# Layer 0 attention: 26 of 96 banks of probabilities transposed by VectorE's blocks and DRAM, the other evictions on ScalarE, one more step of lag

## The chip, the core and the metric

The kernel runs on one core of a Trainium2 chip. The metric is the device time of that core in microseconds (us), as a median over runs. A profile is one execution recorded by the hardware profiler. The core's engines appear in it as PE (TensorE matmuls), PEld (TensorE weight loads), DVE (VectorE), ACT (ScalarE) and POOL (GpSimd); SP is the engine whose queue issues most DMAs. All data are float32.

## The reference

Two transformer layers run over x of shape (4, 256, 512). Each layer is attention and a linear map, each with a residual and a layer norm. The change is in layer 0's attention: 32 query heads of 16 dimensions, 8 key and value heads (4 query heads share one), causal.

```python
q = (x @ Wq + bq).reshape(B, S, 32, 16).transpose(0, 2, 1, 3)      # B, S = 4, 256
k, v = (x @ Wk + bk), (x @ Wv + bv)                                # 8 heads, each repeated 4 times
scores = jnp.einsum('bhqd,bhkd->bhqk', q, k) / 4
scores = jnp.where(causal, scores, NEG)
p = jax.nn.softmax(scores, axis=-1)
out = jnp.einsum('bhqk,bhkd->bhqd', p, v)
x = layernorm(x + out.reshape(B, S, 512) @ Wo + bo)
x = layernorm(x + x @ W0.T + bias)        # W0 from scales and integer codes
```

Layer 1 has 32 query heads and 8 key heads of 128 dimensions with a bias by distance, and a linear map with small integer weights.

## The kernel before

**Layer 0 attention** is 64 steps (b, qt, h, i): 4 sequences b, 2 query tiles qt of 128 rows, 2 halves h, 4 values of i. A step does four heads (G = 4). For qt = 0 a query tile sees one key tile of 128 columns, for qt = 1 two.

`begin0` starts a step. Score matmuls (L482) fill a PSUM tile `sc` (two of these exist). VectorE adds the mask to the diagonal (L487) and takes the negated maximum (L490). ScalarE makes four exponentials with their sums (L274). `divide0` then treats the step before: VectorE takes the reciprocal of its sums (L279), pinned in program order, and GpSimd multiplies the probabilities `pr` by it (L282). There are six `pr` buffers.

`transpose0` brings the probabilities of a step into `prT`, with keys on the partitions, because the output matmul contracts over keys. `transposed_probabilities` does this for each key tile: four TensorE transposes (L297) fill one PSUM bank `pt`, and `evacuate` copies the bank into `prT`. `evacuate` alternates between VectorE (L100) and ScalarE (L102), and all evictions of the layer that call it share that one turn: the transposed inputs xT, x1T, x2T and the attention output oT too. With 32 steps of one bank and 32 of two, layer 0 has 96 such banks. `pt` banks come from a ring of three PSUM banks, which the projections use too.

`end0` acts on the last i of a group (b, qt, h): output matmuls (L531) over `prT` of the whole group, into the bank `o`; after h = 1 `o` is copied to `oT` and `tail0` (output projection L438, norm, linear map L455, norm) is queued.

`run` orders the work. In iteration n it calls, in this order, `before`, `begin0` of step n, `fill`, `transpose0` of step n - lag, and `end0` of step n - lag - more. In layer 0 lag is 3 and more is 2. `fill` advances the queued tails and the projections of the next sequence (L386 keys, L399 queries, L414 values), which are spread over the steps. The order of the calls is a priority for the scheduler that orders each engine's instructions; `keep_in_program_order` pins an instruction to its traced place on its engine, and each engine executes in the order it is given. So the work around the change is: PE takes scores, filling work, transposes and output matmuls in turn, and softmax runs on the other engines a few steps ahead of the transposes.

**Layer 1** (not changed in what it does) sends most of its probabilities another way, `transposed_by_blocks`. VectorE's stream transpose (L308) transposes every 32 x 32 block of `pr` into `blocks`; four DMAs on SP (L314), one for each 32 partitions, write `blocks` to a DRAM tile `way` so that the blocks come to their transposed places; one DMA (L318) reads `way` into `prT`. There writes and read are traced together.

Of the kernel before, what the change touches and what calls it, by code (L numbers as in the profile page):

```python
# [12 lines left out]
F32 = mybir.dt.float32  # L13
# [7 lines left out]
P = 128  # L21
B, S, D = 4, 256, 512
NTT = B * S // P
NC = D // P
NKV, G = 8, 4
# [34 lines left out]
def block_kernel(  # L60
# [20 lines left out]
    nc = tc.nc  # L81
    slopes = [float(s) for s in alibi_slopes()]

    def pool(stack, name, bufs=1, **kw):
        return stack.enter_context(tc.tile_pool(name=name, bufs=bufs, **kw))
# [9 lines left out]
    def evacuate(dst, src):  # L95

        if not last:
            turn[0] ^= 1
        if turn[0] and not last:
            nc.vector.tensor_copy(dst, src)  # L100
        else:
            nc.scalar.copy(dst, src)  # L102
# [20 lines left out]
    a0 = pool(la, "a0", 2, side="right")  # L123
# [7 lines left out]
    def bank_t(name):  # L131
        return ring[0].tile([P, 4, P], F32, tag=ring[1], name=name)
# [156 lines left out]
        pr = sp.tile([P, G, 2 * P], F32, tag="pr", name=f"pr_{name}", bufs=bufs)  # L289
        return nm, sums, pr  # L290

    def transposed_probabilities(name, pr, parts):

        for kt, dst in parts:
            pt = bank_t(f"pt_{name}_{kt}")
            for i in range(G):
                nc.tensor.transpose(pt[:, i, :], pr[:, i, ts(kt, P)], ident)  # L297
            evacuate(dst, pt.rearrange("p i (j q) -> p i j q", q=32))

    def transposed_by_blocks(sp, name, pr, nt, dst):  # L300

        blocks = sp.tile(
            [P, 2, 4, G, 32], F32, tag="blocks", name=f"blocks_{name}", bufs=1
        )
        for kt in range(nt):
            nc.vector.transpose(  # L308
                blocks[:, kt].rearrange("p j h q -> p h j q"),
                pr[:, :, ts(kt, P)].rearrange("p h (j k) -> p h j k", k=32),  # L310
            )
        way = dram.tile([2, 4, 32, 4, G * 32], F32, tag="way", name=f"way_{name}")
        for i in range(4):
            nc.sync.dma_start(  # L314
                way[0:nt, :, :, i, :].rearrange("t j k f -> k (t j) f"),
                blocks[32 * i : 32 * i + 32, 0:nt].rearrange("k t j h q -> k (t j) (h q)"),
            )
        nc.sync.dma_start(  # L318
            dst.rearrange("p t j h q -> p t (j h q)"),
            way[0:nt].rearrange("t j k i f -> (j k) t (i f)"),  # L320
        )
# [174 lines left out]

    open0 = {}
    undivided = []

    def divide0():  # L500


        if undivided:
            divided(*undivided.pop(), True)

    def transpose0(b, qt, h, i, pr):
        name = f"0_{b}_{qt}_{h}_{i}"
        if i == 0:
            open0["p", h] = a0.tile(
                [P, 2, G, 4, 4, 32], F32, tag="prT", name=f"prT0_{b}_{qt}_{h}"  # L510
            )
        prT = open0["p", h]
        transposed_probabilities(
            name,
            pr,
            [(kt, prT[:, kt, i].rearrange("p j n q -> p n j q")) for kt in range(qt + 1)],
        )
        return prT

# [36 lines left out]
    def fill():  # L556
# [6 lines left out]
        [(b, qt, h, i) for b in range(B) for qt in range(2) for h in range(2) for i in range(G)],  # L563
        begin0,
        transpose0,
        end0,
        before0,
        fill,
        lag=3,
        more=2,  # L570
        rest=divide0,
    )
# [179 lines left out]
    s1 = pool(ctx, "s1", 2)  # L752
# [233 lines left out]
    def transpose1(kv, b, qt, pr):  # L986
        name = f"1_{kv}_{b}_{qt}"
        nt = qt + 1
        if kv == NKV - 1:
            prT = s1.tile([P, 2, 4, G, 32], F32, tag="prT", name=f"prT_{name}")  # L990
            transposed_probabilities(
                name, pr, [(kt, prT[:, kt].rearrange("p j h q -> p h j q")) for kt in range(nt)]
            )
            return prT
        prT = s1.tile([P, 2, 4, G, 32], F32, tag="prT", name=f"prT_{name}")
        transposed_by_blocks(s1, name, pr, nt, prT[:, 0:nt])
        return prT

    def end1(kv, b, qt, prT):
# [40 lines left out]
    def fill1():  # L1040
# [9 lines left out]
        [(kv, b, qt) for kv in range(NKV) for b in range(B) for qt in range(2)],  # L1050
        begin1,
        transpose1,
        end1,
        before1,
        fill1,
        lag=1,
# [38 lines left out]
```

## Time and profile before

| | |
|---|---|
| median of 3 runs | 973.45 us (973.12 to 974.13) |
| the profiled execution | 973.24 us |
| its span, first to last instruction | 971.0 us |
| mean granted TensorE clock | 0.993 of full speed |
| layer 0's score matmuls (L482), first and last start | 15.2 and 255.2 us |
| layer 0's output matmuls (L531), first and last start | 40.7 and 277.3 us |
| layer 0's transposes of probabilities (L297), first 300 us | 384 matmuls, 96 banks |
| evictions of these banks | VectorE 43, ScalarE 53 |
| stream transposes (L308), all in layer 1 | 84 |

How to read it: a row of a group names line, engine, operation, the tiles written and read, shapes and count; then the busy time in us, the mean duration of one in ns, and after the second bar the engine's idle time before these instructions with what ended most of it. A matmul's duration includes its latency; successive ones overlap, so their spacing is read from start to start. In a table of windows each line is a stretch of the span, with each engine's busy us and instruction count, then the granted clock, the busy share of the DMA engines and their GB/s.

### The profile page before, as it was taken

Reading aid. Unit: us, or ns where it says so; the run is one execution under the profiler, and the core shown is the slowest. Engines: PE = TensorE matmul, PEld = TensorE weight load, DVE = VectorE, ACT = ScalarE, POOL = GpSimd, SP = SyncE. Lnnn points to the kernel's source line nnn. Section 1 sums busy time; section 2 is a strip of 40 time slices with the busy share of each in tenths; the row PEclk is TensorE's granted clock in tenths of the full one; section 3 lists DMA queues with packets and bytes.
Section 4 is the critical chain, followed back from the end, with each engine's and each line's share of the span. In section 5 each row is a group of like instructions: output and inputs, shape, how many; then the busy total and the mean of one; then the engine's idle time right before and its main releaser. Section 6 shows DMA issues by size and latency. Waiting matters only on the chain.

```text
span 971.0 us, 11394 instructions
## 1 busy us (share of the span) xinstructions
PE 940.3 (97%) x3593; PEld 557.4 (57%) x3593; DVE 619.9 (64%) x1291; ACT 316.5 (33%) x1194; POOL 445.1 (46%) x461
## 2 busy tenths in 40 slices
PE   7999999999899999999999999999999999999996
PEld 5645555554344445666666666666666666666652
DVE  3876867777632446766666676666676667666566
ACT  2664564555511002333212122121222212223442
POOL 2463552644436313443534543534633643556732
PEclk9999999999899999999999999999999999999998
DMA  9300000000020010444443444333453334342001
GB/s 283 138 1 1 0 1 1 1 1 1 1 86 1 22 44 23 108 131 130 117 133 99 116 124 130 119 83 108 124 143 97 113 90 123 99 118 69 1 23 65
DMA packets 76418, 74.45 MB, mean 77 GB/s; under 512 B 5957, under 2 KB 52678, under 8 KB 76358
## 3 DMA queue, kind: packets, MB, share of 16 engines
q1 hardware_dynamic: 75542, 72.28, 26.1%
q10 hardware_dynamic: 816, 1.44, 0.5%
q8 instruction: 29, 0.48, 0.2%
q14 instruction: 31, 0.25, 0.1%
HBM read 49.58 MB, written 24.12 MB: 76 GB/s over the span
## 4 chain that ended last, share of the span: by engine, by line
PE 85%; POOL 7%; DVE 4%; ACT 1%; DMA 1%; issue 1%; SPq 0%; POOLq 0%; DVEq 0%
PE p_q L632 18%; PE po L875 15%; PE sc L962 8%; PE o L1002 8%; PE p_k L632 5%; PE p_v L632 5%; PE o L531 5%; PE sc L482 4%; PE pt L297 4%; PE pq L399 3%; PE py L438 3%; PE pf L455 3%; PE py L836 3%; POOL pr L282 1%; POOL to L861 1%; ACT pr L274 1%
## 5 line engine op out<-in xcount | busy, mean ns | idle before, releaser
L274 ACT ACTIVATE pr<-sc,nm 128x256 f32<-128x256 f32 (+1 forms) x512 | 208.9, 419 | 374.7 <-DVE nm L978 279.2
L282 POOL TENSOR_TENSOR pr<-pr,sums 128x512 f32<-128x512 f32 (+1 forms) x128 | 189.9, 1484 | 240.4 <-DVE sums L279 235.7
L970 DVE SCALAR_TENSOR_TENSOR sc<-table,sc 128x128 f32<-128x128 f32 (+1 forms) x256 | 86.0, 356 | 34.8 <-PE sc L962 32.5
L274 ACT ACTIVATION_READ_ACCUMULATOR pr<-sc,nm 128x1 f32 x512 | 103.5, 202 | 0.0
L962 PEld LDWEIGHTS sc<-kT,qT 128*128 128x128 f32 x512 | 82.4, 191 | 35.1 <-issue 29.2
L962 PE MATMUL sc<-kT,qT 128*128 128x256 f32 (+1 forms) x512 | 95.2, 327 | 0.0
L1002 PE MATMUL o<-prT,v 128*128 128x512 f32 x192 | 92.9, 593 | 0.0
L646 DVE TENSOR_TENSOR qT<-p_q,qT 128x512 f32<-128x512 f32 x96 | 64.6, 686 | 35.6 <-PE p_q L632 34.8
L308 DVE STREAM_TRANSPOSE blocks<-pr 128x512 f32<-128x512 f32 x84 | 57.6, 698 | 45.6 <-POOL pr L282 45.6
L978 DVE TENSOR_REDUCE nm<-sc 128x2 f32<-128x512 f32 (+1 forms) x128 | 70.0, 550 | 1.5
L297 PEld LDWEIGHTS pt<-ident,pr 128*128 128x128 f32 x432 | 49.6, 142 | 33.0 <-issue 18.2
L297 PE MATMUL pt<-ident,pr 128*128 128x128 f32 x432 | 62.8, 280 | 5.7 <-POOL pr L282 5.3
L490 DVE TENSOR_REDUCE nm<-sc 128x4 f32<-128x512 f32 (+1 forms) x64 | 61.0, 953 | 1.1
L482 PE MATMUL sc<-kT,qT 32*128 32x256 f32 (+1 forms) x256 | 59.9, 533 | 1.6 <-ACT pr L274 1.6
L487 DVE TENSOR_TENSOR sc<-sc,causal 128x512 f32<-128x512 f32 x64 | 44.3, 692 | 26.4 <-PE sc L482 26.2
L875 PE MATMUL po<-wo,so 128*128 128x256 f32 x224 | 58.0, 382 | 2.1 <-POOL so L612 2.1
L632 PE MATMUL p_q<-x2T,ws_q 128*128 128x512 f32 x128 | 59.8, 593 | 0.0
L632 PE MATMUL p_q<-xt,ws_q 128*128 128x512 f32 x128 | 57.8, 593 | 1.8 <-POOL ws_q L615 1.8
L875 PE MATMUL po<-wo,o 128*128 128x256 f32 x224 | 57.7, 381 | 0.0
L632 PE MATMUL p_q<-x2T,wq 128*128 128x512 f32 x128 | 57.6, 593 | 0.0
L102 ACT COPY o<-o 128x512 f32<-128x512 f32 x29 | 17.0, 585 | 124.5 <-PE o L1002 124.5
L875 PE MATMUL po<-to,so 128*128 128x256 f32 x224 | 53.3, 381 | 0.9 <-POOL so L615 0.9
(155 smaller groups left out, 1435.6 us busy)
## 6 DMA issues: line engine op xcount, KB each, us to landing
way<-blocks SPq DMA_DIRECT2D x112, 128.0 KB, 2.5
prT<-way SPq DMA_DIRECT2D x28, 512.0 KB, 3.7
wq<-in_L_attn_w_qkv_dram SPq DMA_DIRECT2D x8, 1024.0 KB, 5.3
wo<-in_L_attn_w_o_dram SPq DMA_DIRECT2D x8, 1024.0 KB, 5.4
way<-blocks SPq DMA_DIRECT2D x112, 64.0 KB, 1.8
prT<-way SPq DMA_DIRECT2D x28, 256.0 KB, 2.7
wk<-in_L_attn_w_qkv_dram SPq DMA_DIRECT2D x4, 512.0 KB, 4.0
wv<-in_L_attn_w_qkv_dram SPq DMA_DIRECT2D x2, 1024.0 KB, 6.3
```

The lines of the kernel that those rows point to most:

```text
L274: nc.scalar.activation(pr[:, i, 0:w], sc, AF.Exp, bias=nm[:, i : i + 1], accum_out=sums[:, i : i + 1])
L282: nc.gpsimd.tensor_tensor(pr[:, :, 0:w], pr[:, :, 0:w], sums.unsqueeze(2).to_broadcast([P, G, w]), ALU.mult)
L297: nc.tensor.transpose(pt[:, i, :], pr[:, i, ts(kt, P)], ident)
L482: nc.tensor.matmul(sc[:, j, :, 0:w], qT[rows, i, ts(qt, P)], kT[rows, :, 0:w], start=True, stop=True)
L490: nc.vector.tensor_reduce(nm, scf[:, :, 0:w], AX.X, ALU.max, negate=True)
L632: nc.tensor.matmul(bank, fixed, moving, start=(c == 0), stop=(c == 1))
L646: add = lambda dst, a, b: nc.vector.tensor_tensor(dst, a, b, ALU.add)
L875: nc.tensor.matmul(bank[:, ts(n, HALF)], left[:, c, :], right[:, c, :], start=(c == 0), stop=(c == 1),)
L962: nc.tensor.matmul(sc[:, m, 0:w], qT[:, 2 * j + m, b * S + qt * P : b * S + (qt + 1) * P], kT[:, b * S : b * S + w], start=True, stop=True,)
L970: nc.vector.scalar_tensor_tensor(sc[:, m, 0:w], table[:, 2 * P - w :], slopes[kv * G + 2 * j + m], sc[:, m, 0:w], ALU.mult, ALU.add,)
L978: nc.vector.tensor_reduce(nm[:, 2 * j : 2 * j + 2], sc[:, :, 0:w], AX.X, ALU.max, negate=True)
L1002: nc.tensor.matmul(o, v1[:, 2 * b + kt, ts(kv, P)], prT[:, kt].rearrange("p j h q -> p h j q"), start=(kt == 0), stop=(kt == qt),)
```

## The change

In layer 0, for every (b, qt) from (0, 1) to (2, 1), key tile 0 of some steps no longer goes through TensorE: for qt = 1 the steps with i = 0, 1, 2 (their second key tile stays on TensorE), for qt = 0 the steps with i = 0 and 2. That makes 3 x 2 x 3 + 2 x 2 x 2 = 26 banks. They take `transposed_by_blocks` with one key tile, from two buffers of one tile each (layer 1 keeps one buffer of two tiles). In layer 0 VectorE's transpose is pinned in program order. The four writes are traced at once; the read is returned as a function, which the next step's `transpose0` calls after its own writes, and which is pinned on SP's queue. All other banks except those of (0, 0) are copied by ScalarE alone instead of in turns. The lag is 4 steps instead of 3.

```diff
-    def transposed_probabilities(name, pr, parts):
+    def transposed_probabilities(name, pr, parts, copy=evacuate):
...
-            evacuate(dst, pt.rearrange("p i (j q) -> p i j q", q=32))
+            copy(dst, pt.rearrange("p i (j q) -> p i j q", q=32))
...
-    def transposed_by_blocks(sp, name, pr, nt, dst):
+    def transposed_by_blocks(sp, name, pr, nt, dst, room):
...
-            [P, 2, 4, G, 32], F32, tag="blocks", name=f"blocks_{name}", bufs=1
+            [P, room, 4, G, 32], F32, tag="blocks", name=f"blocks_{name}", bufs=2 // room
...
-            nc.vector.transpose(
+            ins = nc.vector.transpose(
...
+            if room == 1:
+                tc.keep_in_program_order(ins)
...
-        nc.sync.dma_start(
+        return lambda: nc.sync.dma_start(
             dst.rearrange("p t j h q -> p t (j h q)"),
...
+    unread = []
...
     def transpose0(b, qt, h, i, pr):
...
         prT = open0["p", h]
+        rest = range(qt + 1)
+        reads = list(unread)
+        unread.clear()
+        if (0, 0) < (b, qt) < (B - 1, 0) and i in ((0, 2), (0, 1, 2))[qt]:
+            rest = rest[1:]
+            unread.append(transposed_by_blocks(a0, name, pr, 1, prT[:, 0:1, i], 1))
+        for read in reads:
+            tc.keep_in_program_order(read())
+        copy = evacuate if (b, qt) == (0, 0) else nc.scalar.copy
         transposed_probabilities(
-            name,
-            pr,
-            [(kt, prT[:, kt, i].rearrange("p j n q -> p n j q")) for kt in range(qt + 1)],
+            name, pr, [(kt, prT[:, kt, i].rearrange("p j n q -> p n j q")) for kt in rest], copy
         )
         return prT
...
-        lag=3,
+        lag=4,
...
-        transposed_by_blocks(s1, name, pr, nt, prT[:, 0:nt])
+        transposed_by_blocks(s1, name, pr, nt, prT[:, 0:nt], 2)()
```

## The prediction

> **What bounds the kernel now.** The page first, for the whole; then the table of windows, cut at the first score matmul of each (b, qt) stretch of layer 0, for where each engine is full; then PE's order of time; then the rows by form for prices.
>
> ```profile
> PE 940.3 (97%) x3593; PEld 557.4 (57%) x3593; DVE 619.9 (64%) x1291; ACT 316.5 (33%) x1194; POOL 445.1 (46%) x461
> ...
> PE 85%; POOL 7%; DVE 4%; ACT 1%; DMA 1%; issue 1%; SPq 0%; POOLq 0%; DVEq 0%
> ```
>
> PE is busy 97% of the span and is 85% of the chain that ended last. A busy PE need not be at its peak, so I go to the stretches (columns: PE, PEld, DVE, ACT, POOL busy, then the granted clock and DMA). Six of the nine:
>
> ```profile
> 38.60:67.60 29.00, 28.51 (x147) 15.48 (x146) 22.43 (x40) 18.51 (x70) 16.14 (x11) 1.00 0.00 1
> 67.60:101.00 33.40, 33.24 (x166) 18.36 (x166) 22.66 (x48) 18.40 (x79) 13.80 (x14) 1.00 0.01 1
> 101.00:134.00 33.00, 32.52 (x157) 17.34 (x156) 25.92 (x46) 18.06 (x69) 17.46 (x13) 1.00 0.00 1
> ...
> 200.50:230.00 29.50, 28.68 (x142) 13.37 (x142) 20.61 (x44) 17.51 (x75) 13.34 (x13) 1.00 0.00 1
> 230.00:256.00 26.00, 25.14 (x110) 11.31 (x109) 19.99 (x35) 15.95 (x62) 13.39 (x10) 1.00 0.00 0
> 256.00:297.00 41.00, 37.03 (x125) 16.36 (x124) 13.97 (x27) 8.92 (x25) 19.29 (x15) 0.92 0.15 52
> ```
>
> From 38.6 to 134 PE idles 1.1 us in 95.4. VectorE is at 77%, 68% and 79% in these three, ScalarE at 55 to 64%, and the DMA engines stand still. PE sets the pace wherever the change takes banks away; VectorE is next. The last stretch is different: PE idles 4.0 us and the clock falls.
>
> PE's timeline gives what a bank of four transposes really holds of PE (start, us, what):
>
> ```profile
> 140.38 1.04 PE L297 MATMUL pt<-ident,pr 128*128 128x128 f32 x8
> 141.35 0.70 PE L482 MATMUL sc<-kT,qT 32*128 32x256 f32 x4
> ...
> 146.54 0.66 PE L297 MATMUL pt<-ident,pr 128*128 128x128 f32 x4
> 147.12 0.69 PE L482 MATMUL sc<-kT,qT 32*128 32x256 f32 x2
> ```
>
> Eight hold it 141.35 - 140.38 = 0.97 us, four 147.12 - 146.54 = 0.58. So one bank beside another costs about 0.39 to 0.44 (start to start of single transposes is 0.109 us, four are 0.436), and a bank that is a group of its own costs 0.58, because the change of operand shape is paid too. The rows of the first 300 us:
>
> ```profile
> L297 PE MATMUL pt<-ident,pr 128*128 128x128 f32 x384 | 56.0, 280 | 3.6 <-POOL pr L282 3.2 <-DVE v L422 0.2
> L102 ACT COPY prT<-pt 128x512 f32<-128x512 f32 x53 | 30.9, 591 | 30.2 <-PE pt L297 30.1
> L100 DVE COPY prT<-pt 128x512 f32<-128x512 f32 x43 | 29.0, 675 | 7.8 <-PE pt L297 7.8
> ```
>
> Its mean of 280 ns is latency, not spacing; 384 matmuls are 96 banks.
>
> **The change part by part.** *PE loses 26 banks.* In (0,1), (1,1), (2,1) the blocks take key tile 0 of i = 0, 1, 2 for two h: 3 x 6 = 18 banks, each beside a second bank that stays: 18 x 0.436 = 7.8 us. In (1,0), (2,0) they take the only bank of i = 0, 2: 2 x 4 = 8 groups: 8 x 0.58 = 4.6 us. Together 12.5 us, all on PE, at full clock, in the stretches where PE hardly idles. This is the main term: -12.5.
>
> *A rule against it.* The Trainium skill, "VectorE: DVE Perf Modes", sections "The three transpose paths" and "Rules for kernel authors", says to give a 128x128 transpose to TensorE if PSUM may receive it, and prices one (bf16) at 390 ns there and 311 ns on VectorE, in 32x32 blocks only. By those prices a bank of four would free 1.56 us of PE, 40 us in all, and cost VectorE 1.24 us instead of a 0.60 us copy, +17 us on the engine next in load. This case's row for a whole bank on VectorE is shorter:
>
> ```profile
> L308 DVE STREAM_TRANSPOSE blocks<-pr 128x512 f32<-128x512 f32 x82 | 56.2, 698 | 44.2 <-POOL pr L282 44.1
> ```
>
> The row is layer 1's; it covers a bank in 698 ns, and in VectorE's timeline the next instruction starts 0.60 us after it, as after a copy. I use 0.58 and 0.436 for PE and 0.60 for VectorE.
>
> *VectorE.* It takes 26 transposes and gives up nearly all of its 43 prT copies, since every eviction after (0,0) goes to ScalarE; the four banks of (0,0) that may fall to it stay. Some 39 x 0.60 = 23 us go, 26 x 0.60 = 16 us come. Within the five changed stretches about half of their 64 banks were VectorE's, so there it is nearly a swap: same work in less time. (1,1) then runs at about 25.9/30.4 = 85% and (0,1) at 85%. In b = 3 (24 banks, no blocks) VectorE loses about 7 us of the 41 in its two stretches.
>
> *ScalarE.* 96 - 26 - 4 = 66 copies for 53: +13 x 0.59 = 7.7 us, nearly all in b = 3, where it goes from 33.5 of 55.5 us to some 40. A copy queued there delays the exponentials behind it, and through them the score tiles PE waits for; at 72% load I count that as covered.
>
> *Wait for the probabilities.* The pinned transpose heads VectorE's queue until GpSimd has divided; behind it wait the next step's mask and maximum, so exponentials and scores. Layer 1's row shows 44.2 us of such waits in 82. Here the tile is four steps old (about 15 us), while its reciprocal is issued one step on and the division takes 1.1 or 1.9 us, so I take zero.
>
> *DMAs.* Each bank adds four writes and a read on SP, idle in layer 0 between its loads near 23 us and the value weights at 282 us; engines at 0.00. Layer 1's same sizes:
>
> ```profile
> way<-blocks SPq DMA_DIRECT2D x112, 64.0 KB, 1.8
> prT<-way SPq DMA_DIRECT2D x28, 256.0 KB, 2.7
> ```
>
> Issue of four writes takes 1.8 us on SP (timeline of layer 1), landing 1.8 more, then the read waits for its turn one step on (3.8 us) and lands in 2.7: some 8 us after the transpose. The last block of a group is i = 2, and its output matmul is traced three steps later, over 11 us. Cover about 3 us or more; nothing on the path. The bounds: 0, and the rival below.
>
> *Lag 4.* Moves each transpose one step later behind the scores. It removes GpSimd waits of PE: 1.0 us near 227 and, at the drain, where PE waits 2.60 us at 256.8 for a division, one more group of eight transposes (0.97 us) stands in front. -2.0. Six pr buffers leave one step of slack instead of two: zero.
>
> *New stalls.* Stretch (3,1), with VectorE at 77% and little filling work, idles PE 0.86 us in 26; before that with 79% and filling work 0.48 in 33. At 85% I charge the worse rate, doubled, to the three qt = 1 stretches (some 90 us): 90 x 2 x 0.033 = 6 as the upper bound, zero as the lower, and take 2, nearer the filled stretch. VectorE's relief in b = 3 and two copies (1.2 us) fewer ahead of the last softmax may give some back; I leave that in the range.
>
> Sum: -12.5 - 2.0 + 2.0 = -12.5 us. On the profiled execution of 973.24 (span 971.0 and 2.2 around it): 960.7. The median before is 0.2 above that execution, so 960.9.
>
> **The clock at the drain.** In 252 to 264 the granted clock is 0.76 and in 264 to 276 0.95:
>
> ```profile
> 252.00:264.00 12.00, 9.40 (x42) 4.55 (x42) 8.09 (x16) 6.00 (x20) 4.33 (x3) 0.76 0.00 1
> ```
>
> That is 0.24 x 12 + 0.05 x 12 = 3.5 us of lost clock, less half of what fell into the wait, about 2.9. The Trainium skill, "TensorE: Matmul & The Clock Gate" (Part 4 and "Why this matters for your kernels"), allows idle gaps to about 3 us and says transposes do not count as busy. The gap here is 2.60 us, shorter than allowed, and mostly transposes precede it. By the gap alone a 1.6 us wait is safe and 2.9 us come back; by the second sentence an extra group of transposes does not help. I take no gain and keep -2.9 for the range.
>
> **The rivals.**
> 1. *VectorE and the ScalarE queue become the bound* (0.14). The stalls reach their upper bound of 6 and lag 4 gains nothing: -12.5 + 6 = -6.5, 967. For: 85% in order. Against: PE idles only 0.5 us at 79%.
> 2. *The drain clears* (0.16). The short wait vanishes, the clock stays up: another -0.6 - 2.9, and VectorE's relief in b = 3 repays about 1.2: 956.2.
> 3. *Slower: the round trip through DRAM ends late* (0.05). Ten groups hold blocks, and each group's output matmul holds PE for the read. With 14.5 us gained, it decides at 1.45 us per group. If SP's pinned read waits behind the next step's writes, and these for a VectorE running a step and a half late, 8 us become 13.5, about 2 late: +20, net +5.5, 979. Against: VectorE's lag behind PE is seldom over 3 us here.
> 4. *No effect* (0.03): PE's time refills with waits for exponentials. 973. Against: such waits of PE's score matmuls come to 1.6 us.
>
> The likeliest (0.62) has its own range, 957 to 964.
>
> **How the numbers follow.** A measurement tells about 0.2% (1.9 us) from no change. Faster is cases 1, 2 and the likeliest, 0.92; same 0.03; slower 0.05. For 8 in 10 the range takes the likeliest, most of case 2 and the better part of case 1: 954.5 to 967.5.
>
> **What would show it.** L297 falls from 384 to 280 matmuls in layer 0, the prT copies of VectorE from 43 to about 4, ScalarE's rise to about 66; 26 more stream transposes and 26 more reads of 256 KB. The stretches (0,1) to (2,1) shrink by 2 to 3 us each with PE idle below 1 us; the chain stays on PE. I am wrong if output matmuls (L531) wait on a DMA, if PE waits for exponentials or banks grow by several us, or if the drain grows by more than it should.

## The result and the profile after

The changed kernel takes 973.75 us (median of 12 runs, 971.51 to 975.65) against 973.08 us before: a ratio of 1.0005, 95% interval 0.9997 to 1.0014. I had forecast 960.9 us; nothing that can be measured was gained. What each engine has to do changed as forecast. The rows of the first 300 us and the page's DMA rows after:

```profile
L297 PE MATMUL pt<-ident,pr 128*128 128x128 f32 x280 | 40.2, 277 | 1.1 <-POOL pr L282 1.1
L298 ACT COPY prT<-pt 128x512 f32<-128x512 f32 x62 | 35.3, 596 | 45.1 <-PE pt L297 45.1
L308 DVE STREAM_TRANSPOSE blocks<-pr 128x512 f32<-128x512 f32 x26 | 18.1, 698 | 0.1
```

```profile
way<-blocks SPq DMA_DIRECT2D x216, 64.0 KB, 1.8
prT<-way SPq DMA_DIRECT2D x54, 256.0 KB, 2.7
```

PE does 104 matmuls fewer (384 to 280), ScalarE 62 prT copies by the new line L298 and four more by `evacuate`, and VectorE 26 stream transposes at 698 ns that wait for nothing (0.1 us). Writes and reads land in 1.8 and 2.7 us as in layer 1. But:

```profile
PE 932.1 (96%) x3489; PEld 546.9 (56%) x3489; DVE 613.3 (63%) x1273; ACT 324.4 (33%) x1212; POOL 444.2 (46%) x461
...
PE 82%; POOL 7%; DVE 5%; ACT 4%; issue 2%; DMA 1%; SPq 0%; POOLq 0%; DVEq 0%; ACTq 0%
```

PE works 8.2 us less and the span is 0.5 us longer: ScalarE's part of the chain grew from 1 to 4%. Where this falls is shown by the table of windows, cut at the first score matmul of each (b, qt) stretch. These are (1,0), (1,1), (2,1), the first part of (3,1), and the rest; the last cut is at 253.3 us, while scores of (3,1) still run to 261.1, so the last two lines are not the windows of before:

```profile
64.30:98.80 34.50, 32.04 (x151) 16.50 (x150) 22.64 (x47) 18.11 (x78) 13.04 (x13) 0.95 0.36 88
98.80:133.80 35.00, 32.37 (x133) 15.56 (x132) 25.38 (x45) 18.48 (x71) 17.89 (x13) 0.95 0.27 67
...
166.30:202.60 36.30, 33.67 (x135) 16.01 (x134) 25.44 (x45) 18.55 (x71) 17.91 (x13) 0.91 0.26 64
...
229.70:253.30 23.60, 19.75 (x89) 8.19 (x88) 18.29 (x32) 17.73 (x67) 13.84 (x10) 1.00 0.00 1
253.30:297.50 44.20, 43.11 (x157) 20.58 (x158) 13.03 (x27) 13.41 (x34) 19.98 (x16) 0.96 0.14 48
```

Stretch (1,1) took 33.0 us before with PE idle 0.5 us at full clock. Now, with less for PE to do, it takes 35.0 us with PE idle 2.6 us and the granted clock at 0.95. VectorE's load in it is 73%, not the 85% I feared. Stretch (3,1) lost most: its scores start from 229.7 to 261.1 us, 31.4 us, for 25.2 us before (230.0 to 255.2). PE's own list of waits (15 to 283 us; total, times, longest) names what it waits for, before and after:

```profile
PE sc L482 <- ACT pr L274: 1.6, 4, 0.4
```

```profile
PE sc L484 <- ACT pr L274: 12.2, 14, 1.7
```

Two pairs of these waits stand near 120 and 188 us. Here is ScalarE near 120 us, first before the change, then after (the sums between the exponentials are left out):

```profile
119.73 1.08 ACT L102 COPY prT<-pt 128x512 f32<-128x512 f32 x2
121.46 0.58 ACT L102 COPY oT<-o 128x512 f32<-128x512 f32 x1 [0.64 <-PE o L531]
121.94 0.48 ACT L274 ACTIVATE pr<-sc,nm 128x256 f32<-128x256 f32 x1
```

```profile
120.21 0.59 ACT L298 COPY prT<-pt 128x512 f32<-128x512 f32 x1
120.68 0.51 ACT L274 ACTIVATE pr<-sc,nm 128x256 f32<-128x256 f32 x1
...
121.14 0.50 ACT L274 ACTIVATE pr<-sc,nm 128x256 f32<-128x256 f32 x1
...
121.59 0.51 ACT L274 ACTIVATE pr<-sc,nm 128x256 f32<-128x256 f32 x1
...
122.04 0.51 ACT L274 ACTIVATE pr<-sc,nm 128x256 f32<-128x256 f32 x1
...
122.49 0.63 ACT L102 COPY oT<-o 128x512 f32<-128x512 f32 x1
```

And PE at the same places, before and after:

```profile
119.50 1.91 PE L531 MATMUL o<-prT,v 128*32 128x512 f32 x8
121.34 1.13 PE L482 MATMUL sc<-kT,qT 32*128 32x512 f32 x4
122.40 3.70 PE L438 MATMUL py<-wop,oT 128*128 128x512 f32 x8
```

```profile
117.14 1.91 PE L544 MATMUL o<-prT,v 128*32 128x512 f32 x8
120.38 1.13 PE L484 MATMUL sc<-kT,qT 32*128 32x512 f32 x4 [1.34 <-ACT pr L274]
122.70 1.12 PE L484 MATMUL sc<-kT,qT 32*128 32x512 f32 x2 [1.19 <-ACT pr L274]
123.75 5.40 PE L440 MATMUL py<-wop,oT 128*128 128x512 f32 x8
```

Before, ScalarE took oT 0.05 us after the output matmuls had ended (121.41), and PE went from one group of scores straight to the output projection `py`. After, the output matmuls end at 119.05, but oT stands behind a prT copy and the four exponentials of one more step and starts at 122.49, 3.44 us late. PE cannot do `py`; what stands ahead of it is half of the next scores, which wait for those same exponentials. Then `py` takes 5.40 us for 3.70: the trace has half the clock granted from 124.6 us, for 3.41 us. The same happens near 187 and 250 us: oT of (1,0), (2,0) and (3,0), the three on ScalarE, is late by 3.44, 3.44 and 3.23 us; the five on VectorE are not.

So theory A was that the softmax chain through VectorE had become the bound; the rivals were the longer lag (B), ScalarE's copies as such (C), PE's own order (D), and the pinned block transposes (E). Out of the first runs came F: it is the place of oT in ScalarE's queue.

### The profile page after: what moved, and what is told of

Same layout as the page of the kernel before. It is cut to its first block, busy times and chain, and to the rows that moved or that the text cites. A ratio compares the mean times of both kernels' runs of the same rounds, so it can differ in the third digit from the quotient of the medians.

```text
span 971.5 us, 11444 instructions
## 1 busy us (share of the span) xinstructions
PE 932.1 (96%) x3489; PEld 546.9 (56%) x3489; DVE 613.3 (63%) x1273; ACT 324.4 (33%) x1212; POOL 444.2 (46%) x461
## 4 chain that ended last, share of the span: by engine, by line
PE 82%; POOL 7%; DVE 5%; ACT 4%; issue 2%; DMA 1%; SPq 0%; POOLq 0%; DVEq 0%; ACTq 0%
PE p_q L645 18%; PE po L888 15%; PE sc L975 8%; PE o L1015 8%; PE p_k L645 5%; PE p_v L645 5%; PE sc L484 4%; PE py L440 4%; PE o L544 3%; ACT pr L274 3%; PE pf L457 3%; PE py L849 3%; PE pt L297 2%; PE pq L401 2%; POOL to L874 1%
## 5 line engine op out<-in xcount | busy, mean ns | idle before, releaser
L274 ACT ACTIVATION_READ_ACCUMULATOR pr<-sc,nm 128x1 f32 x512 | 105.9, 207 | 0.0
L308 DVE STREAM_TRANSPOSE blocks<-pr 128x512 f32<-128x512 f32 x110 | 75.7, 698 | 45.7 <-POOL pr L282 45.6
L484 PE MATMUL sc<-kT,qT 32*128 32x256 f32 (+1 forms) x256 | 62.3, 535 | 12.5 <-ACT pr L274 12.2
L888 PEld LDWEIGHTS po<-to,so 128*128 128x128 f32 x224 | 42.2, 190 | 16.3 <-issue 8.8
L297 PEld LDWEIGHTS pt<-ident,pr 128*128 128x128 f32 x328 | 37.2, 141 | 24.3 <-issue 15.4
```

The lines of the kernel that those rows point to most:

```text
L274: nc.scalar.activation(pr[:, i, 0:w], sc, AF.Exp, bias=nm[:, i : i + 1], accum_out=sums[:, i : i + 1])
L308: ins = nc.vector.transpose(blocks[:, kt].rearrange("p j h q -> p h j q"), pr[:, :, ts(kt, P)].rearrange("p h (j k) -> p h j k", k=32),)
L484: nc.tensor.matmul(sc[:, j, :, 0:w], qT[rows, i, ts(qt, P)], kT[rows, :, 0:w], start=True, stop=True)
L888: nc.tensor.matmul(bank[:, ts(n, HALF)], left[:, c, :], right[:, c, :], start=(c == 0), stop=(c == 1),)
```

## The experiments

All ratios are to the kernel before, on the same chip. "oT late" is worked out from each trace: the start of each oT copy minus the end of the last output matmul ahead of it, summed over the eight. "Clock lost" is (1 - mean granted clock) x span, an upper bound for what the falls cost, the ends of the span included. The profile is one execution, so the last two columns show direction, not a law. Executions of one kernel differ with the clock: four of e2's six took 962.1 to 962.5 us at a mean clock of 0.997 to 0.998, the other two 967.6 and 967.9 us at 0.992.

| run | what it is | us | ratio (95%) | oT late | clock lost |
|---|---|---|---|---|---|
| before | | 973.1 to 973.5 | 1 | 1.0 | 6.8 |
| after | the change | 973.75 | 1.0005 (0.9997 to 1.0014) | 10.5 | 10.7 |
| e1 | before, lag 4 | 972.03 | 0.9989 (0.9983 to 0.9996) | 2.4 | 1.9 |
| e7 | e1, ScalarE copies | 982.54 | 1.0113 (1.0092 to 1.0134) | 8.4 | 6.9 |
| e12 | e7, oT on VectorE | 970.43 | 0.9979 (0.9969 to 0.9989) | 1.1 | 2.9 |
| e13 | e1, oT on VectorE | 974.19 | 1.0012 (1.0005 to 1.0018) | 4.5 | 2.9 |
| e16 | e1, oT one step late | 985.51 | 1.0125 (1.0112 to 1.0138) | 9.1 | 7.9 |
| e2 | after, copies in turns | 962.42 | 0.9908 (0.9885 to 0.9931) | 4.7 | 2.9 |
| e8 | after, oT on VectorE | 963.23 | 0.9908 (0.9892 to 0.9924) | 1.2 | 7.7 |
| e14 | e2, oT on VectorE | 966.01 | 0.9922 (0.9903 to 0.9942) | 7.5 | 9.7 |
| e15 | e2, no block transposes | 962.39 | 0.9895 (0.9878 to 0.9911) | 3.3 | 3.8 |
| e9 | e2, lag 3 | 968.09 | 0.9952 (0.9938 to 0.9965) | 1.0 | 1.9 |
| e3 | after, lag 3 | 968.99 | 0.9958 (0.9946 to 0.9971) | 3.6 | 4.8 |
| e4 | after, 104 transposes more | 970.86 | 0.9977 (0.9967 to 0.9987) | 4.1 | 2.9 |
| e5 | after, not pinned | 983.77 | 1.0118 (1.0102 to 1.0134) | 12.6 | 16.7 |
| e10 | after, turns in b = 3 | 971.05 | 0.9983 (0.9973 to 0.9992) | 7.9 | 4.8 |

Two things in the traces go with the table. First, PE's order: wherever oT on ScalarE is 2.4 us late or more, PE takes half of the next group of four score matmuls ahead of `py` and the other half after it. This is so in three places of the changed kernel, e5, e7 and e16, in two of e10, in one of e3 and e4, and nowhere else. Second, within layer 0 the falls of the clock are stretches of 3.41 or 6.83 us at half speed. Half their length, the most that they can cost there, is 3.4 us before, 8.5 after, 0 in e1, e2, e9, e12 and e13, 3.4 in e7 and 5.1 in e16; but also 5.1 in e8, with oT in time at the first two places, so not every fall hangs on oT.

**e1_lag4: the lag alone.**

```diff
-        lag=3,
+        lag=4,
```

> The kernel before with the lag at 4, nothing else. Theory A (the softmax chain through VectorE, with only two score tiles, has become what PE waits for once its transposes are fewer): the lag alone changes little, within 2 us of 973.1. Rival B (the longer lag orders PE so that score matmuls stand closer together, and this is the loss): 5 to 12 us slower. My prediction's step (lag 4 gains 2 us): 971.

1.5 us faster by the medians of its comparison (972.03 and 973.54). B falls, and my step for the lag (-2.0) was about right in size.

**e2_turns: evictions in turns again, blocks kept.**

```diff
-        copy = evacuate if (b, qt) == (0, 0) else nc.scalar.copy
+        copy = evacuate
```

> The changed kernel with the evictions of layer 0 in turns between VectorE and ScalarE again, the block transposes kept. Theory A, with VectorE as the late engine: about 31 more copies of 0.60 us in VectorE's queue, 3 to 8 us slower than the changed kernel (977 to 982). Rival C (copies between the exponentials on ScalarE delay the score tiles): 3 to 8 us faster (966 to 971).

962.42 us, 11.3 less than the changed kernel, and better than both kernels. VectorE gets more copies and the time falls: A in its VectorE form is out. C is right on the part of the change, not yet on why.

**e3_lag3: the change with lag 3** (`lag=4` to `lag=3`).

> The changed kernel with the lag back at 3. Rival B (the lag costs): 4 us or more faster, 970 or less. Theory A: within 3 us of 973.7, the waits for exponentials stay at 10 us or more.

968.99, as B said, though e1 had just shown that the lag by itself costs nothing. In its trace oT of (1,0) and (2,0) is in time (0.05 us) and only that of (3,0) is 3.23 us late. So B's number came out for another reason: the lag moved the scheduler's order.

**e4_twice: PE's 104 transposes given back.**

```diff
...
-            for i in range(G):
+            for i in list(range(G)) * times:
...
-            name, pr, [(kt, prT[:, kt, i].rearrange("p j n q -> p n j q")) for kt in rest], copy
+            name, pr, [(kt, prT[:, kt, i].rearrange("p j n q -> p n j q")) for kt in rest], copy, 2 if (0, 0) < (b, qt) < (B - 1, 0) and i in ((1, 3), (0, 1, 2))[qt] else 1
```

> The changed kernel in which PE does the four transposes of 26 of the remaining banks twice, into the same bank: the 104 matmuls that the change removes are given back to PE (104 x 0.109 = 11.3 us) with no work for any other engine. Theory A (PE has as much waiting as it has lost work): at most 4 us slower, the waits for exponentials shrink. Rival D (PE is still the bound and lost its gain elsewhere in its own order): about 11 us slower, 985.

2.9 us faster than the changed kernel, with 11.3 us more work for PE. D, by which it would be about 11 us slower, is out. It is no clean measure of PE's slack: the longer transposes moved oT forward in ScalarE's order (late by 0.32 us at two places).

**e7_act_only: the evictions alone, no blocks.**

```diff
...
+            evacuate if (b, qt) == (0, 0) else nc.scalar.copy,
...
-        lag=3,
+        lag=4,
```

> The kernel before with lag 4 and all prT evictions after (0, 0) on ScalarE, all transposes on PE, no blocks. Lag 4 alone gave 972.0. Theory C1 (copies of prT in ScalarE's queue hold back the exponentials by themselves): 4 to 10 us slower than that, 976 to 982. Theory C2 (they only hurt together with fewer transposes on PE, which leave score matmuls close together, and with the clock that falls on the waits): within 2 us of 972.

982.54, 10.5 us over e1, which differs from it by the evictions alone. This is the loss, at its full size, without any block. C2 falls: it does not take fewer transposes on PE. The number is C1's; that its cause is not C1's is shown by e8 and e12.

**e5_unpinned: VectorE's block transposes free to move.**

```diff
-            if room == 1:
-                tc.keep_in_program_order(ins)
```

> The changed kernel with VectorE's block transposes not pinned, so that the scheduler may move them away from the masks. Rival E (a pinned transpose ahead of a mask is what makes the exponentials late): 5 us or more faster, 968 or less, with waits for exponentials under 8 us. Theory C (ScalarE's copies and the clock): within 3 us of 973.7.

983.77, 10 us worse, so E is out. Neither theory gave this. Here oT is late by 4.16, 4.20 and 3.23 us and the clock loss is the largest of all: another order, the same symptom, larger.

**e8_oT_vector: only oT moved, to VectorE.**

```diff
-            evacuate(oT.rearrange("p i q -> p (i q)"), o)
+            turn[0] ^= 1; nc.vector.tensor_copy(oT.rearrange("p i q -> p (i q)"), o)
```

> The changed kernel with only the eight oT evictions always on VectorE (the turn of the others is kept). Theory C3 (it is oT queued on ScalarE behind two steps of exponentials and a copy, near 122 and 190 us, that leaves PE without its output projection and lets the clock fall): the clock stays up there, about 5 to 10 us faster, 964 to 968. Theory C1: within 2 us of 973.7, since the prT copies stay.

963.23. Three copies that change engine bring 10.5 us; all prT copies stay on ScalarE. C1 falls, C3 (which I then called F) stands. A few other copies moved in ScalarE's order too, so e12, below, is the cleaner pair.

**e10_turns_in_b3: turns for b = 3 only** (`copy = evacuate if (b, qt) == (0, 0) or b == B - 1 else nc.scalar.copy`).

> The changed kernel with evictions in turns for (0, 0) and for b = 3 only; in the stretches with blocks they stay on ScalarE. If the loss sits in the stretches with blocks (waits near 67, 120, 137, 188, 206 us and three of the four falls of the clock): at most 4 us faster than 973.7. If it sits in b = 3 (24 banks, waits near 232 to 253 us): 8 us or more faster, near 963.

971.05, 2.7 less than the change. It mends the third oT (0.68 us late for 3.23) and leaves the other two at 3.44: a third of the places, a quarter of the loss.

**e12_act_only_oT: e7 with e8's edit.**

> The run with lag 4 and ScalarE copies only (no blocks; 982.5), now with oT evicted by VectorE. Theory F (what ScalarE's copies cost is oT, queued there 2.4 to 3.2 us late behind exponentials in three places): nearly all of the 10.5 us comes back, 971 to 974. Theory C1 (the 24 or more prT copies there hold back the exponentials everywhere): at most 3 us come back, 979 or more.

970.43, 12.1 us less than e7: all of its 10.5 us come back, and 1.6 more. Some 88 prT copies on ScalarE, with oT in time, cost nothing. In the traces, up to the last scores ScalarE's order in the two runs differs by the three oT copies alone, and PE's by the split of one score group in each of the three places.

**e13_lag4_oT: the control, e1 with e8's edit.**

> Control: the kernel before with lag 4 (972.0), oT evicted by VectorE. Theory F: oT is at most 0.8 us late there, so nothing or up to 2 us is gained, 970 to 972.5. If VectorE is simply the better place for oT whatever the order, 5 us or more are gained, 967 or less.

974.19, 2.2 us worse. VectorE is not the better engine for oT as such; here it makes oT later (1.5 us in two places). F's own number, 970 to 972.5, missed.

**e14_turns_oT: e2 with e8's edit.**

> The changed kernel with evictions in turns (962.4) and oT on VectorE too. Theory F: there oT is late by 1.7 us in two places, which come back, less what VectorE's queue costs: 959 to 962. If VectorE has become the bound: 964 or more.

966.01 by the median, 3.6 over e2, and not the gain that F gave. The runs overlap, though (962.28 to 968.01 for 962.06 to 967.88), and so do the intervals of the ratios. The medians differ with the clock: e14's fastest run has 0.997, the others 0.990 to 0.995. oT is 2.85 us late in two places, on VectorE this time, and PE does not split its scores there. So this run shows neither a bound on VectorE nor a cost of lateness on that engine.

**e15_turns_no_blocks: VectorE's block transposes left out.** A tile filled once is written instead, so key tile 0 of the 26 banks holds zeros; the DMAs stay.

```diff
...
-        blocks = sp.tile(
+        blocks = filled[0] if room == 1 else sp.tile(
...
-        for kt in range(nt):
+        for kt in range(nt if room > 1 else 0):
...
```

> The changed kernel with evictions in turns (962.4) in which VectorE's block transposes are left out: the writes send a tile that is filled once, so key tile 0 of the 26 banks holds zeros. It frees VectorE of 26 x 0.60 = 15.6 us. If the block transposes ahead of the masks cause what the blocks fall short of 12.5 us: 2 to 5 us faster, 957 to 960. If not: within 1.5 us of 962.4.

962.39 for 962.42. Taking 15.6 us of work from VectorE changes nothing in the time within the width of its runs (961.4 to 964.8). In its trace the waits for exponentials are smaller (4.4 us for 7.3), but one fall of the clock stands at 185.0 us.

**e16_late_oT: the loss made by hand.** In the kernel before with lag 4, oT waits for the newest exponentials.

```diff
...
-        nc.scalar.activation(
+        newest[:] = [nc.scalar.activation(
...
-            evacuate(oT.rearrange("p i q -> p (i q)"), o)
+            with tc.issue_after(newest[0].ins): evacuate(oT.rearrange("p i q -> p (i q)"), o)
...
-        lag=3,
+        lag=4,
```

> The kernel before with lag 4 (972.0), in which each oT copy has to wait, on its own engine if that is ScalarE, for the newest exponentials traced: in three places it goes behind one more step of exponentials, as in the changed kernel; ScalarE's queue is else the same. Theory F (late oT copies are the loss): 6 to 11 us slower, 978 to 983, oT 2 to 3 us late in the three places. If the lateness of oT is only a sign of something else: at most 3 us slower, 975 or less.

985.51, 13.5 us over e1 and more than the 6 to 11 expected. In the trace of layer 0, ScalarE's order differs from e1's by three swaps and by nothing else. In e1 oT of (1,0) starts at 124.88 us, ahead of four exponentials. In e16 it stands behind them (the first of the four is shown):

```profile
125.52 0.47 ACT L274 ACTIVATE pr<-sc,nm 128x256 f32<-128x256 f32 x1
...
127.33 0.59 ACT L102 COPY oT<-o 128x512 f32<-128x512 f32 x1
```

The scheduler answered on PE by putting half of the next scores ahead of `py`, as in the changed kernel. PE in e1, and in e16:

```profile
124.58 1.13 PE L482 MATMUL sc<-kT,qT 32*128 32x512 f32 x4 [0.46 <-ACT pr L274]
125.64 3.70 PE L438 MATMUL py<-wop,oT 128*128 128x512 f32 x8
```

```profile
124.97 1.13 PE L482 MATMUL sc<-kT,qT 32*128 32x512 f32 x4 [0.45 <-ACT pr L274]
127.50 1.12 PE L482 MATMUL sc<-kT,qT 32*128 32x512 f32 x2 [1.40 <-ACT pr L274]
128.55 3.70 PE L438 MATMUL py<-wop,oT 128*128 128x512 f32 x8
...
134.84 1.12 PE L482 MATMUL sc<-kT,qT 32*128 32x512 f32 x2
```

In e16 `py` starts 3.58 us after the scores instead of 1.06: 2.5 us more, of which PE waits 1.40 for exponentials and spends 1.05 on the half group of scores. Taking that half early wins nothing. The other half follows at 134.84 us and holds PE for 1.05 us as well, as long as the whole group of four in e1 (1.06). So at the next sequence's first scores e16 is 2.90 us behind e1 (137.35 for 134.45), after 0.39 before the swap. The three places lose 2.5, 2.4 and 2.5 us in this way, and two falls of the clock, 6.83 and 3.41 us at half speed, cost 5.1: together 12.6 of the 12.9 us between the two profiled executions. F is shown.

**e9_turns_lag3: e2 with lag 3.**

> The changed kernel with evictions in turns (962.4) and lag 3. If lag 3 keeps oT in time and the waits for the division and the DRAM reads stay near the 6 us seen with lag 3 before: 959 to 964. If these waits decide: 965 or more.

968.09, with a wide spread (963.2 to 974.2). oT is in time; PE still waits for exponentials (3.8 us for e2's 7.3), and now also for divisions (3.2 us, one of 2.60) and the DMAs through DRAM (2.4 us). The profiled execution, 963.5 us at a clock of 0.998, is one of the fastest. The runs near the median have 0.993, about 5 us more of lost clock, and no trace shows where. So lag 4 is the better lag for the blocks, by 5.7 us of the medians, but why stays open. e2 and e8 stay the best kernels that I have.

## Why the prediction was wrong, step by step

- **PE loses 26 banks: -12.5.** Right. The clean pair is e1 and e2, where the clock does not fall in layer 0 (page rows):

```profile
PE 940.9 (97%) x3593; PEld 556.2 (57%) x3593; DVE 621.5 (64%) x1291; ACT 316.6 (33%) x1194; POOL 444.9 (46%) x461
```

```profile
PE 924.8 (96%) x3489; PEld 544.9 (57%) x3489; DVE 627.9 (65%) x1304; ACT 309.7 (32%) x1181; POOL 445.0 (46%) x461
```

  PE's busy time falls by 16.1 us. By the starts in the traces, the transposes hold it 13.7 us less and the output matmuls 3.2 us less, as fewer transposes cut them apart (18 groups for 23); the rest takes some 0.7 more.
- **New stalls: +2.** Too small: PE's idle time between the first score and the last output matmul rises by 6.6 us (5.8 to 12.4), past my upper bound of 6. So the blocks bring 9.6 us (e1 to e2), 8.8 (e7 to after) and 7.2 (e12 to e8). PE's waits for exponentials rise by 5.5 us in the first pair (1.8 to 7.3) and 5.0 in the last (2.8 to 7.8), even with oT mostly in time. That these waits come of score groups standing closer together on PE, with two score tiles, is argued and not shown. VectorE's transposes have a part in them (4.4 us without, in e15) that did not show in the time.
- **VectorE: a swap.** Right as far as the time shows (e15). By the price in the Trainium skill, "VectorE: DVE Perf Modes", section "The three transpose paths", my estimate for this step was 17 us; the row's 698 ns was the better guide. The same page's advice in "Rules for kernel authors", to keep such transposes on TensorE, does not hold here (e1 to e2: -9.6).
- **Wait for the probabilities, DMAs: 0.** Right at lag 4; at lag 3 the reads begin to show (3.4 us of waits in e3).
- **Lag 4: -2.0.** Alone it gave -1.5, in part by luck. The waits for divisions (3.2 us) went, as forecast. The fall of the clock at the drain went too (3.4 us at most), for which I had taken no gain; but PE's work took about 3 us more with the new order.
- **ScalarE: "A copy queued there delays the exponentials behind it, and through them the score tiles PE waits for; at 72% load I count that as covered."** This is the step that failed: 0 forecast, +10.5 measured (e1 to e7; +11.3 from e2 to after). The load argument holds for the 88 prT copies (e12). I looked at what the copies delay *behind* them and at the mean load, and not at what else uses that queue: the three oT copies on it. With the added copies the order puts oT behind one more step of exponentials, and PE's output projection hangs on oT. PE then takes half of the next scores first, which wait for the same exponentials; the split costs it another 1.05 us, and in some places the clock falls (e16).
- **The clock.** I priced it at the drain only. It fell at 70, 124, 189 and 254 us instead, just after new waits. By the mean clock the upper bound of the loss rose from 6.8 to 10.7 us.
- **The rivals.** Rival 4, to which I gave 0.03, was nearest: "PE's time refills with waits for exponentials. 973." Those waits grew from 1.6 to 12.2 us, which I had also named as a sign of being wrong. It did not say why they would grow. Rival 1 named ScalarE's queue (967), but its load, not a place in its order.

The sum as the runs give it, from before by e1 and e7 to after: lag -1.5, evictions +10.5, blocks -8.8; together 0.2. By e2 instead of e7 it is lag -1.5, blocks -9.6, evictions +11.3. Each sum must come out, since its steps lead from one kernel to the other; what the runs tell is the sizes.

## What to carry to other kernels

When copies are moved to another engine, list what else stands in that engine's order and which of it releases the bound engine: a copy that feeds a long matmul group must not come to stand behind a step of softmax, however low the mean load. Compare the compiled order of that one instruction before and after, since small edits (a lag, a pin, a second transpose) moved it here by up to 3 us and the time by 3 to 10. A regression that an edit "cures" may be cured by the reordering; making the suspected fault by hand in the old kernel, as e16 does, tells the two apart.

## What I had not expected of the hardware

The clock of PE fell after waits that are shorter than I allowed for. In the changed kernel two waits of 1.34 and 1.19 us within 3.6 us, with score matmuls between, were followed by a fall, and `py` took 5.40 us for 3.70:

```profile
118.00:130.00 12.00, 9.48 (x30) 3.94 (x27) 5.88 (x11) 6.66 (x26) 5.68 (x3) 0.86 0.24 58
```

PE was busy 79% of this window and got 0.86 of the clock. The Trainium skill, "TensorE: Matmul & The Clock Gate", section "Why this matters for your kernels", asks for no idle gap over about 3 us; here no gap came near that. In e15 a single wait of 1.27 us, from 182.5 us, stands before a fall at 185.0.

These runs give no threshold in its place. e2 has a single wait of 1.94 us before 119.6 us, at full clock. In e16 the same two waits of 0.45 and 1.40 us come twice, with the same work around them: near 126 us the clock stayed full, near 197 us it fell for 6.83 us. What decides between the two is not shown.
